# Block 0 ahead of the routers' tables, vectors loaded during layer 0's pages, and first pages of layer 1 cut into pieces inside the fused pass

## The chip, the cores and the metric

One core of a Trainium2 chip runs the whole program. The metric is the device time of one execution in microseconds, without a profile; the median of several runs is given. A profile of one further execution shows where the time goes.

## The reference

Two layers, each of a graph step and a mixture of experts, on 128 graphs of 64 nodes with 256 features (8192 tokens), all in float32:

```python
# layer 0: graph step, then a "lattice" mixture with the best 6 of 64 experts
x = x + gnn0(layernorm(x), adj)       # agg = eps*h + adj@h;  W1 -> rmsnorm -> silu -> W2 (256 -> 1024 -> 256)
x = x + ffn0(layernorm(x))            # sum over 6 experts of score * (h @ lattice[e]), out_w, layernorm
# layer 1: graph step, then a mixture with the best 2 of 8 experts
x = x + gnn1(layernorm(x), adj)       # layer_norm, adj@h@W_rel + h@W_root, relu
x = x + ffn1(layernorm(x))            # relu(h@W1[e]+b1)@W2[e]+b2, weighted with a softmax of the two logits
```

The tokens are routed: only the chosen experts are computed for a token.

## The kernel before

The tokens are worked on in NB = 32 blocks of 256 (two tiles of 128 rows). There are four passes, one after the other, and three seams between them.

1. **Layer 0's graph step** (lines 636 to 870). For each block: load x and its adjacency (`load0`), layer norm (`norm_a`, `norm_s`, `norm_e`, `norm_b`), `aggregate`, four `hidden` parts, `rms`, `scale`, `project`, and then the routing: logits, `choose`, `count`, `place`, and `send`, which scatters the rows of a token to the places of its six experts in a table in DRAM. A `Router` object (r0 for layer 0, r1 for layer 1) keeps small tables for this: its constructor writes them with GpSimd and converts them on VectorE.
2. **Layer 0's pages** (lines 875 to 975). A page is up to 128 rows of one expert. Twelve early pages first, then pairs of pages: `fetch` a page from the table (12 pairs ahead), `flip` (transpose, copy out on ScalarE), `apply` (multiply with the expert's matrix, scale on VectorE, `reply`: scatter the answers to DRAM with an indirect DMA of GpSimd). While the first 64 pairs run, ScalarE's queue also writes filler rows (`fill_end`).
3. **The fused pass** (lines 983 to 1284). For each block: load the six answers per token (`load_y`) and the saved rows (`load3`), sum the answers on TensorE (`mixture`), the output projection, layer norms, layer 1's graph step, and layer 1's routing with `choice`, `count1`, `slots`, `place1` and `send1`. `READY` says for how many first blocks `load_y` need not wait for the last replies; `fold` adds two of the six answers on VectorE in later blocks.
4. **Layer 1's pages** (lines 1287 to 1360). A page is up to 256 rows of one of 8 experts. `fetch1` loads the page, its expert's W1 with b1 (`pw`) and b2; `flip1` transposes; `up` and `down` are the two matrix products; `down` also does the softmax weight and adds the answer to the output with two indirect DMAs that accumulate (`r1.add`). Which expert and which rows a page has is read from a page table that VectorE computes after the last block (`page_table`). The first `FIRST` = 3 pages, numbered -3 to -1, are the first full pages of experts 0 to 2 and need no table. The tiles come from a pool with a fixed number of buffers: four for the page (`px`), three for `pw`, four for b2.

Within a pass, the order on TensorE, VectorE and ScalarE is the program's own: `staggered(n, stages)` takes steps s, and in each step goes through the list of stages, running stage f with lag l for block s - l. So what stands in the list above something else is ahead of it in each engine's order, and an engine takes its instructions strictly in that order. SP's and GpSimd's instructions are placed by the framework's scheduler, which can pull a load forward. SP and ScalarE both issue DMAs; the framework gives these DMAs eight completion semaphores in turn, and a DMA that gets one in use waits until the DMA before it on that semaphore has landed.

The lines that matter:

- Start: the routers are built at lines 616 to 618, ahead of everything of block 0. `load0(0)`, `load0(1)` (lines 659, 660), epsilon, `eye` (epsilon times the identity, line 664), W1 (line 666), b1, and at line 825 a load of ScalarE's function table. After that the `staggered` list with block 0's normalization at lag -1.
- Seam between layer 0's pages and the fused pass: lines 988 to 998 load three weight matrices, Wg and six vectors (ln_g, ln_b, gamma, beta, bg, bias) on ScalarE's queue, and VectorE adds bias to bg. SP loads the answers at line 1010.
- Seam between the fused pass and layer 1's pages: the list ends with `place1` (one `send1`; the other three stand at lag 4), then `page_table`, then the pages with `stages = (-2, fetch1), (0, flip1), (1, down), (0, up)`.

Of the kernel before, what the change touches and what calls it, by code (L numbers as in the profile page):

```python
# [9 lines left out]
F32 = mybir.dt.float32  # L10
# [3 lines left out]
ENG = mybir.EngineType  # L14
# [5 lines left out]
P = 128  # L20
# [509 lines left out]
def two_layer_gnn_moe_kernel(ctx: ExitStack, tc: tile.TileContext, a: dict, out: bass.AP):  # L530
# [16 lines left out]
    READY = 5  # L547
# [92 lines left out]
    with tc.tile_pool(name="c0", bufs=1) as c0, \  # L640
# [10 lines left out]
        r0.begin(counts, work, route)  # L651
# [166 lines left out]
        def load_lattice(b):  # L818
# [6 lines left out]
        nc.scalar.preload_act_table_set("natural_log_exp_and_others")  # L825
# [6 lines left out]
            (-1, norm_a),  # L832
# [3 lines left out]
            (-1, norm_s),  # L836
            (-1, norm_e),
# [6 lines left out]
            (-1, norm_b),  # L844
# [6 lines left out]
            (-1, aggregate),  # L851
# [63 lines left out]
    with tc.tile_pool(name="wx0", bufs=3, reuse_waits="tile") as wx, \  # L915
# [5 lines left out]
        ring = [wx.tile([P, KD, C], F32, name="pxT", bufs=5)]  # L921

# [44 lines left out]
        staggered(mean_pages, stages)  # L967
# [14 lines left out]
    wx = ctx.enter_context(tc.tile_pool(name="wx1", bufs=2, side="right", reuse_waits="tile"))  # L982
    with tc.tile_pool(name="c3", bufs=1, reuse_waits="tile") as c3, \
# [19 lines left out]
        FIRST = 3  # L1003
# [215 lines left out]
        A, H, R, S = chain(output), chain(choice), chain(residual), chain(slots)  # L1219
        staggered(NB, (  # L1220
# [11 lines left out]
            (4, lambda b: send1(b, 1)),  # L1232
# [9 lines left out]
            (1, flip_h),  # L1242
            (2, R),
# [9 lines left out]
            (4, lambda b: send1(b, 2)),  # L1253
# [9 lines left out]
            (4, lambda b: send1(b, 3)),  # L1263
            (1, convolve_a),
            (3, count1),
            (-3, fold),
# [6 lines left out]
            (2, flip3),  # L1273
            (1, convolve_b),
            (2, gate1),
            (0, A),
# [6 lines left out]
        r1.page_table(work.tile([P, 512], F32, name="scratch", bufs=1))  # L1283


    with tc.tile_pool(name="pt4", bufs=2, space=PSUM, reuse_waits="tile") as pt_pool, \
            tc.tile_pool(name="ph4", bufs=4, space=PSUM, reuse_waits="tile") as ph_pool, \
            tc.tile_pool(name="py4", bufs=2, space=PSUM, reuse_waits="tile") as py_pool:
        PG = 2 * P
        pages = {i: dict() for i in range(-FIRST, r1.pages)}  # L1290
        regs = {}

        likely = r1.likely_pages - FIRST

        def load1(i, e):
            Q = pages[i]
            Q["w"] = w = wx.tile([P, F1W], F32, name="pw", bufs=3)
            nc.sync.dma_start(out=w, in_=fw1[ds(e, 1)].rearrange("o p f -> p (o f)"))
            Q["b2"] = b2 = wx.tile([P, D], F32, name="pb2", bufs=4)
            nc.sync.dma_start(out=b2, in_=a["L1_ffn_b2"][ds(e, 1), :].to_broadcast([P, D]))  # L1300

        def fetch1(i):
            Q = pages[i]
            Q["x"] = x = wx.tile([P, 2, W], F32, name="px", bufs=4)
            if i < 0:
                if i == -FIRST:
                    regs["first"] = r1.load_first(0, ENG.SP)
                r1.fetch_first(regs["first"][i + FIRST], x)
                load1(i, i + FIRST)
                return  # L1310
            if i % 4 == 0 or i == likely:
                regs["row"], regs["esp"] = r1.load(0, i, ENG.SP), r1.load(1, i, ENG.SP)
            r1.fetch(i, regs["row"][i % 4], x)
            load1(i, regs["esp"][i % 4])

        def flip1(i):
            Q = pages[i]
            pt = pt_pool.tile([P, KD, PG], F32, name="pt")
            ops.transpose(pt, Q["x"])
            Q["xT"] = xT = wx.tile([P, KD, PG], F32, name="pxT")  # L1320
            nc.scalar.copy(xT, pt)

        def up(i):
            Q = pages[i]
            w = Q["w"]
            Q["hid"] = hid = wx.tile([P, KF, PG], F32, name="phid")
            for c in range(KF):
                ph = ph_pool.tile([P, PG], F32, name="ph")
                for k in range(KD):
                    nc.tensor.matmul(ph, lhsT=w[:, k * F1 + c * P:k * F1 + (c + 1) * P], rhs=Q["xT"][:, k, :],  # L1330
                                     start=(k == 0), stop=(k == KD - 1))
                nc.scalar.activation(hid[:, c, :], ph, AF.Relu, bias=w[:, KD * F1 + c:KD * F1 + c + 1], scale=1.0)  # L1332

        def down(i):
            Q = pages[i]
# [4 lines left out]
            e = regs["e"][i % 4] if i >= 0 else i + FIRST  # L1340

            p = wx.tile([P, 2], F32, name="p")
            nc.scalar.activation(p, Q["x"][:, :, D + 1], AF.Exp)  # L1343
            nc.vector.tensor_scalar(p, p, 1.0, None, op0=ALU.add)  # L1344
            nc.vector.reciprocal(p, p)
            py = py_pool.tile([P, 2, D], F32, name="py")
            y = wx.tile([P, 2, D], F32, name="py_s")
            for t in range(2):
                for c in range(KF):
                    nc.tensor.matmul(py[:, t, :], lhsT=Q["hid"][:, c, ts(t, P)],  # L1350
                                     rhs=fw2[:, ds(e, 1), c, :].rearrange("p o d -> p (o d)"),
                                     start=(c == 0), stop=(c == KF - 1))
            nc.vector.tensor_add(y, py, Q["b2"].unsqueeze(1).to_broadcast([P, 2, D]))  # L1353
            for t in range(2):
                nc.vector.tensor_scalar(y[:, t, :], y[:, t, :], p[:, t:t + 1], None, op0=ALU.mult)
                r1.add(i, Q["x"][:, t, :], y[:, t, :])
# [37 lines left out]
```

## Time and profile before

| | us |
|---|---|
| median of 3 runs without a profile | 2033.03 (2029.64 to 2033.41) |
| the profiled execution, whole | 2284.81 |
| its span, first to last instruction | 2283.0 |
| mean granted clock of TensorE in it | 0.946 |

The four passes in the span, read from the order of time: layer 0's graph step to about 740, layer 0's pages to about 1379, the fused pass to about 1753, layer 1's pages to the end. Busy time in the whole span: PE 87%, PEld 74%, DVE 51%, ACT 44%, POOL 51%.

The profile names the engines PE (TensorE's matmuls), PEld (its weight loads), DVE (VectorE), ACT (ScalarE), POOL (GpSimd), SP (SyncE). A `q` behind a name is the engine's queue that issues DMAs. A line of the view of time gives start and duration in us, the engine, the source line, the instruction, `out<-in` by the program's names without buffer numbers, how many were merged, and in brackets how long the engine was idle before and what released it. In a view of waits the three numbers are total us, count and the longest.

Two rows of the page that the steps below use:

```profile
L386 POOL DMA_INDIRECT out_x<-py_s,px x138 | 215.5, 1561 | 296.4 <-DMA out_x<-py_s,px 235.5
L1330 PE MATMUL ph<-pxT,pw 128*128 128x256 f32 x1104 | 251.3, 381 | 0.7 <-issue 0.7
```

The first is the scatter-add of layer 1's answers: 138 of them (two for each of 69 pages), 1561 ns each, with POOL idle for 296.4 us before them, most of it until an earlier one had landed. The second is `up`: 16 records a page.

### The profile page before, as it was taken

The numbers are of one execution on the slowest core, as the hardware profiler recorded it, in microseconds if no ns is written. First come the engines' busy times: TensorE is split into PE (matmuls) and PEld (weight loads), VectorE is DVE, ScalarE is ACT, GpSimd is POOL, SyncE is SP. The second block draws the span as 40 slices with busy tenths as digits, with TensorE's granted clock in tenths as the row PEclk, the third lists the DMA queues.
The fourth block names the chain that finished last, engine by engine and source line by source line (L and its number), as shares of the span: only waits on it lengthen the run. The fifth ranks groups of instructions, "written<-read, shape, count | busy, mean of one in ns | idle before, by whom it ended". The sixth has DMA issues, their size and how long they took to land. (4 is left out here: it accounts for less than half of the span.)

```text
span 2283.0 us, 36780 instructions
## 1 busy us (share of the span) xinstructions
PE 1975.4 (87%) x10324; PEld 1692.3 (74%) x10324; DVE 1162.4 (51%) x4165; ACT 1007.1 (44%) x2033; POOL 1171.0 (51%) x1134
## 2 busy tenths in 40 slices
PE   7988888888874677888788787999998999999996
PEld 6867777777763566667667666878886888888885
DVE  5868878777876222222222223878996222222221
ACT  5867677676761112121111112666665333333332
POOL 0445566556556666666666662334545344444443
PEclk9999999999996898999989888999998999999998
DMA  4323444444345787755555527999872766766674
GB/s 111 98 100 126 143 144 139 140 140 134 111 159 188 220 246 208 224 176 173 175 172 174 155 73 275 313 305 311 303 227 96 176 168 158 167 163 162 159 163 98
DMA packets 282558, 397.88 MB, mean 174 GB/s; under 512 B 56024, under 2 KB 236392, under 8 KB 282352
## 3 DMA queue, kind: packets, MB, share of 16 engines
q1 hardware_dynamic: 202880, 246.61, 37.0%
q0 software_dynamic: 64416, 136.14, 19.9%
q10 hardware_dynamic: 15056, 12.69, 1.7%
q8 instruction: 92, 1.51, 0.3%
q14 instruction: 114, 0.93, 0.1%
HBM read 222.84 MB, written 176.64 MB: 175 GB/s over the span
## 5 line engine op out<-in xcount | busy, mean ns | idle before, releaser
L369 POOL DMA_INDIRECT r0x<-xs,r0row x384 | 396.9, 1034 | 343.2 <-DVE xs L328 132.8
L954 PE MATMUL py<-lat,pxT 128*128 x1616 | 426.9, 411 | 110.7 <-ACT pxT L941 68.9
L376 POOL DMA_INDIRECT r0y<-px x404 | 391.8, 970 | 227.6 <-DVE px L958 118.9
L954 PEld LDWEIGHTS py<-lat,pxT 128*128 128x128 f32 x1616 | 317.7, 207 | 165.3 <-ACT pxT L941 77.7
L958 DVE TENSOR_SCALAR px<-py,px 128x256 f32<-128x256 f32 x404 | 170.9, 478 | 446.9 <-remote 154.3
L386 POOL DMA_INDIRECT out_x<-py_s,px x138 | 215.5, 1561 | 296.4 <-DMA out_x<-py_s,px 235.5
L941 ACT COPY pxT<-pt 128x512 f32<-128x512 f32 x202 | 113.9, 588 | 515.1 <-remote 214.3
L1332 ACT ACTIVATE phid<-ph,pw 128x256 f32<-128x256 f32 x276 | 130.6, 473 | 323.3 <-issue 186.2
L1330 PE MATMUL ph<-pxT,pw 128*128 128x256 f32 x1104 | 251.3, 381 | 0.7 <-issue 0.7
L1350 PE MATMUL py<-fw,phid 128*128 (+1 forms) x1104 | 249.9, 379 | 0.0
L753 PE MATMUL ps<-lat 128*128 128x256 f32 x1024 | 245.5, 390 | 0.0
L720 PE MATMUL ph<-lat 128*128 128x256 f32 x1024 | 237.5, 390 | 5.1 <-DVE lat L742 2.8
L1330 PEld LDWEIGHTS ph<-pxT,pw 128*128 128x128 f32 x1104 | 210.9, 191 | 30.0 <-issue 1.1
L720 PEld LDWEIGHTS ph<-lat 128*128 128x128 f32 x1024 | 196.9, 195 | 35.7 <-issue 7.0
L1350 PEld LDWEIGHTS py<-fw,phid 128*128 128x128 f32 x1104 | 204.4, 190 | 25.2 <-issue 0.3
L753 PEld LDWEIGHTS ps<-lat 128*128 128x128 f32 x1024 | 198.5, 196 | 26.8
L369 POOL DMA_INDIRECT r1x<-xs,r1row x128 | 137.7, 1076 | 106.5 <-ACT hn L1105 49.8
L939 PE MATMUL pt<-ident,px 128*128 128x128 f32 x808 | 130.7, 283 | 15.7 <-DMA px<-r0x 10.4
L939 PEld LDWEIGHTS pt<-ident,px 128*128 128x128 f32 x808 | 106.6, 148 | 41.3 <-issue 18.5
L723 ACT ACTIVATE lat<-ph,c_L_gnn_b 128x256 f32<-128x256 f32 x256 | 101.2, 471 | 58.5 <-PE ph L720 39.7
L1353 DVE TENSOR_TENSOR py_s<-py,pb 128x512 f32<-128x512 f32 x69 | 47.7, 691 | 155.3 <-PE py L1350 155.3
L1344 DVE TENSOR_SCALAR p<-p 128x2 f32<-128x2 f32 x69 | 11.7, 170 | 224.6 <-ACT p L1343 224.6
(307 smaller groups left out, 2927.2 us busy)
## 6 DMA issues: line engine op xcount, KB each, us to landing
px<-r0x SPq DMA_DIRECT2D x404, 129.0 KB
y<-r0y SPq DMA_DIRECT2D x64, 768.0 KB
pw<-in_L_ffn_W1b SPq DMA_DIRECT2D x69, 514.0 KB
px<-r1x SPq DMA_DIRECT2D x69, 258.0 KB
x<-x SPq DMA_DIRECT2D x64, 256.0 KB
pb<-in_L_ffn_b SPq DMA_DIRECT2D x69, 128.0 KB
r0x<-r0filler ACTq DMA_DIRECT2D x64, 129.0 KB
lat<-in_x SPq DMA_DIRECT2D x32, 256.0 KB
```

The lines of the kernel that those rows point to most:

```text
L369: i = self.nc.gpsimd.indirect_dma_start(out=self.table[:, :], out_offset=bass.IndirectOffsetOnAxis(ap=row[:, t, k:k + 1], axis=0), in_=xs[ ...
L376: d = self.nc.gpsimd.indirect_dma_start(out=self.answer[:, :], out_offset=bass.IndirectOffsetOnAxis(ap=x[:, self.D:self.D + 1].bitcast(I32 ...
L386: i, d = f"{self.name}add{i}", self.nc.gpsimd.indirect_dma_start(out=self.total[:, :], out_offset=bass.IndirectOffsetOnAxis(ap=x[:, self.D ...
L720: nc.tensor.matmul(ph[:, c, :], lhsT=w1[:, k, ts(2 * j + c, P)], rhs=B["aggT"][:, k, :], start=(k == 0), stop=(k == KD - 1))
L753: nc.tensor.matmul(B["po"][:, t, :], lhsT=B["hT"][:, c, ts(t, P)], rhs=w2[:, c, :], start=False, stop=(t == T - 1 and c == KH - 1))
L939: nc.tensor.transpose(pt[:, k, ts(q, P)], Q["px"][:, q, ts(k, P)], ident)
L941: nc.scalar.copy(xT[:, :, :n * P], pt[:, :, :n * P])
L954: nc.tensor.matmul(py[:, q, :], lhsT=xT[:, k, ts(q, P)], rhs=lat[:, ds(regs["e"][(2 * j + q) % 4], 1), k, :].rearrange("p o d -> p (o d)") ...
L958: nc.vector.tensor_scalar(px[:, q, :D], py[:, q, :], px[:, q, D + 1:D + 2], None, op0=ALU.mult)
L1330: nc.tensor.matmul(ph, lhsT=w[:, k * F1 + c * P:k * F1 + (c + 1) * P], rhs=Q["xT"][:, k, :], start=(k == 0), stop=(k == KD - 1))
L1332: nc.scalar.activation(hid[:, c, :], ph, AF.Relu, bias=w[:, KD * F1 + c:KD * F1 + c + 1], scale=1.0)
L1350: nc.tensor.matmul(py[:, t, :], lhsT=Q["hid"][:, c, ts(t, P)], rhs=fw2[:, ds(e, 1), c, :].rearrange("p o d -> p (o d)"), start=(c == 0), s ...
```

## The change

It does four things, in three places.

1. The routers are built after block 0's normalization and aggregation instead of before. Block 0's stages are called once by hand, and the list skips them for block 0 (`rest`). ScalarE's function table is loaded before W1's load is issued, and block 1's loads stand after W1 and b1.
2. The six vectors go into tables of r0 that are no longer needed once layer 0's page table exists, and are loaded during pairs 8 to 13 of layer 0's pages on ScalarE's queue; bias is added at pair 18. `READY` becomes 6, and the condition of `fold` is adapted so that it holds for the same blocks.
3. `FIRST` becomes 4. The functions of a page move ahead of the fused pass and are split: `up` can do a part of its four chunks, `down` one of its two tiles, and `share` and `answer` hold what `down` did on ScalarE, VectorE and GpSimd. Page -4 and the flip and up of page -3 stand in the list of the fused pass at fixed steps, with PSUM tiles borrowed from that pass (`places_of`). After the pass come the page table and then the rest of pages -4 and -3 and the up of page -2.
4. In the last two blocks `place1` sends all four rows of the block at once.

```diff
-    READY = 5
+    READY = 6
...
-    r0 = Router(tc, const, small, dram, N, D, E0, K0, T, P, 14 * P, 4, "r0", 3)
-    W = r0.W
-    r1 = Router(tc, const, small, dram, N, D, E1, 2, T, 2 * P, N, 4, "r1", 1, total=out, like=r0)
-
+    W = D + 2
...
         load0(0)
-        load0(1)
         epsilon = c0.tile([P, 1], F32, name="epsilon")
         nc.scalar.dma_start(out=epsilon, in_=rows_of(a["L0_gnn_epsilon"]))
         eye = c0.tile([P, P], F32, name="eye")
-        nc.vector.tensor_scalar(eye, ident, epsilon, None, op0=ALU.mult)
+        nc.scalar.preload_act_table_set("natural_log_exp_and_others")
...
         b1 = load_columns(c0, "L0_gnn_b1")
+        load0(1)
...
-        nc.scalar.preload_act_table_set("natural_log_exp_and_others")
+        norm_a(0)
+        norm_s(0)
+        nc.vector.tensor_scalar(eye, ident, epsilon, None, op0=ALU.mult)
+        norm_e(0)
+        norm_b(0)
+        aggregate(0)
+        rest = lambda f: lambda b: f(b) if b else None
+
+        r0 = Router(tc, const, small, dram, N, D, E0, K0, T, P, 14 * P, 4, "r0", 3)
+        r1 = Router(tc, const, small, dram, N, D, E1, 2, T, 2 * P, N, 4, "r1", 1, total=out, like=r0)
+        assert W == r0.W
+        r0.begin(counts, work, route)
...
+        over = dict(ln_g=r0.map.rearrange("p j e -> p (j e)")[:, :D], ln_b=r0.nth.rearrange("p j e -> p (j e)")[:, :D],
+                    gamma=r0.end[:, :KD], beta=r0.delta[:, :KD], bg=r0.alloc[:, :E1], gbias=r0.none[:, :E1])
+
+        def load_vectors(j):
+
+            if 8 <= j < 14:
+                name, v = (("ln_g", "L0_ffn_ln_g"), ("ln_b", "L0_ffn_ln_b"), ("gamma", "L1_gnn_ln_gamma"),
+                           ("beta", "L1_gnn_ln_beta"), ("bg", "L1_ffn_bg"), ("gbias", "L1_ffn_bias"))[j - 8]
+                with nc.allow_non_contiguous_dma(reason="small vector"):
+                    nc.scalar.dma_start(out=over[name], in_=a[v].rearrange("(c p) -> p c", p=P) if j in (10, 11)
+                                        else rows_of(a[v]))
+            if j == 18:
+                nc.vector.tensor_add(over["bg"], over["bg"], over["gbias"])
...
-        staggered(mean_pages, stages)
+        staggered(mean_pages, (*stages, (0, load_vectors)))
...
+    FIRST = 4
...
+    def up(i, lo=0, hi=KF):
...
+    def down(i, e, tiles=(0, 1)):
...
+    def share(i):
+
+        Q = pages[i]
+        Q["p"] = p = wx.tile([P, 2], F32, name="p")
+        nc.scalar.activation(p, Q["x"][:, :, D + 1], AF.Exp)
+        nc.vector.tensor_scalar(p, p, 1.0, None, op0=ALU.add)
+        nc.vector.reciprocal(p, p)
+
+    def answer(i):
+        Q = pages[i]
+        y, p = wx.tile([P, 2, D], F32, name="py_s"), Q["p"]
+        nc.vector.tensor_add(y, Q["py"], Q["b2"].unsqueeze(1).to_broadcast([P, 2, D]))
+        for t in range(2):
+            nc.vector.tensor_scalar(y[:, t, :], y[:, t, :], p[:, t:t + 1], None, op0=ALU.mult)
+            r1.add(i, Q["x"][:, t, :], y[:, t, :])
...
-        ln_g = load_rows(c3, "L0_ffn_ln_g")
-        ln_b = load_rows(c3, "L0_ffn_ln_b")
-        gamma = load_columns(c3, "L1_gnn_ln_gamma")
-        beta = load_columns(c3, "L1_gnn_ln_beta")
+        ln_g, ln_b, gamma, beta, bg = (over[x] for x in ("ln_g", "ln_b", "gamma", "beta", "bg"))
...
-        bg = load_rows(c3, "L1_ffn_bg")
-        gbias = load_rows(c3, "L1_ffn_bias")
-        nc.vector.tensor_add(bg, bg, gbias)
...
-            if b > READY + 2:
+            if b > READY + 1:
...
         def place1(b):
-            send1(b, 0)
+            for i in range(4 if b >= NB - 2 else 1):
+                send1(b, i)
...
+        def ahead(*work):
+
+            def do(b):
+                for n, f in work:
+                    if n == b - NB:
+                        f()
+            return do
...
             (1, flip_h),
+            (4, ahead((-4, lambda: up(-4, 0, 2)))),
             (2, R),
...
             (3, count1),
+            (4, ahead((-3, lambda: down(-4, 0, (0,))), (-2, lambda: up(-3)))),
...
             (2, flip3),
+            (4, ahead((-5, lambda: flip1(-4)), (-3, lambda: flip1(-3)))),
             (1, convolve_b),
             (2, gate1),
+            (4, ahead((-8, lambda: fetch1(-4)), (-7, lambda: fetch1(-3)), (-6, lambda: fetch1(-2)),
+                      (-4, lambda: up(-4, 2)), (-3, lambda: down(-4, 0, (1,))))),
...
         r1.page_table(work.tile([P, 512], F32, name="scratch", bufs=1))
+        share(-4)
+        answer(-4)
+        flip1(-2)
+        down(-3, 1)
+        up(-2)
+        share(-3)
+        answer(-3)
...
-        stages = (-2, fetch1), (0, flip1), (1, down), (0, up)
-        staggered(likely, stages, -FIRST)
+        stages = (-2, fetch), (0, then(flip1)), (1, finish), (0, then(up))
+        staggered(likely, stages, -2)
```

In the pages' loop `finish` does what `down` did (`share`, `down`, `answer`, and for pages 0 to 7 the filler), and `then` and `fetch` skip what pages -4 to -2 have already had.

More of the change, by code (lines that the diff above doesn't have):

```diff
@@ L650, in two_layer_gnn_moe_kernel @@
         blocks = [dict() for _ in range(NB)]
-        r0.begin(counts, work, route)
         def load0(b):
@@ L831, in two_layer_gnn_moe_kernel @@
             (-2, lambda b: load0(b) if b > 1 else None),
-            (-1, norm_a),
+            (-1, rest(norm_a)),
             (0, lambda b: hidden(b, 0)),
@@ L835, in two_layer_gnn_moe_kernel @@
             (2, residual_s),
-            (-1, norm_s),
-            (-1, norm_e),
+            (-1, rest(norm_s)),
+            (-1, rest(norm_e)),
             (4, lambda b: send(b, 3)),
@@ L843, in two_layer_gnn_moe_kernel @@
             (2, residual_b),
-            (-1, norm_b),
+            (-1, rest(norm_b)),
             (4, lambda b: send(b, 4)),
@@ L850, in two_layer_gnn_moe_kernel @@
             (0, square_sum),
-            (-1, aggregate),
+            (-1, rest(aggregate)),
             (-1, load_late),
@@ L982, in two_layer_gnn_moe_kernel, with load1 @@
     wx = ctx.enter_context(tc.tile_pool(name="wx1", bufs=2, side="right", reuse_waits="tile"))
+    PG = 2 * P
+    FIRST = 4
+    pages = {i: dict() for i in range(-FIRST, r1.pages)}
+    regs = {}
+    likely = r1.likely_pages - FIRST
+    def load1(i, e):
+        Q = pages[i]
+        Q["w"] = w = wx.tile([P, F1W], F32, name="pw", bufs=3)
+        nc.sync.dma_start(out=w, in_=fw1[ds(e, 1)].rearrange("o p f -> p (o f)"))
+        Q["b2"] = b2 = wx.tile([P, D], F32, name="pb2", bufs=4)
+        nc.sync.dma_start(out=b2, in_=a["L1_ffn_b2"][ds(e, 1), :].to_broadcast([P, D]))
@@ new lines, in fetch1 @@
+    def fetch1(i):
+        Q = pages[i]
+        Q["x"] = x = wx.tile([P, 2, W], F32, name="px", bufs=4)
+        if i < 0:
+            if i == -FIRST:
+                regs["first"] = r1.load_first(0, ENG.SP)
+            r1.fetch_first(regs["first"][i + FIRST], x)
+            load1(i, i + FIRST)
+            return
+        if i % 4 == 0 or i == likely:
+            regs["row"], regs["esp"] = r1.load(0, i, ENG.SP), r1.load(1, i, ENG.SP)
+        r1.fetch(i, regs["row"][i % 4], x)
+        load1(i, regs["esp"][i % 4])
@@ new lines, in flip1 @@
+    def flip1(i):
+        Q = pages[i]
+        pt = Q["pt"](0)
+        ops.transpose(pt, Q["x"])
+        Q["xT"] = xT = wx.tile([P, KD, PG], F32, name="pxT")
+        nc.scalar.copy(xT, pt)
+    def up(i, lo=0, hi=KF):
+        Q = pages[i]
+        w = Q["w"]
+        if lo == 0:
+            Q["hid"] = wx.tile([P, KF, PG], F32, name="phid")
+        hid = Q["hid"]
+        for c in range(lo, hi):
+            ph = Q["ph"](c)
+            for k in range(KD):
+                nc.tensor.matmul(ph, lhsT=w[:, k * F1 + c * P:k * F1 + (c + 1) * P], rhs=Q["xT"][:, k, :],
+                                 start=(k == 0), stop=(k == KD - 1))
+            nc.scalar.activation(hid[:, c, :], ph, AF.Relu, bias=w[:, KD * F1 + c:KD * F1 + c + 1], scale=1.0)
@@ new lines, in down @@
+    def down(i, e, tiles=(0, 1)):
+        Q = pages[i]
+        if 0 in tiles:
+            Q["py"] = Q["py"](0)
+        py = Q["py"]
+        for t in tiles:
+            for c in range(KF):
+                nc.tensor.matmul(py[:, t, :], lhsT=Q["hid"][:, c, ts(t, P)],
+                                 rhs=fw2[:, ds(e, 1), c, :].rearrange("p o d -> p (o d)"),
+                                 start=(c == 0), stop=(c == KF - 1))
+    def share(i):
+        Q = pages[i]
+        Q["p"] = p = wx.tile([P, 2], F32, name="p")
+        nc.scalar.activation(p, Q["x"][:, :, D + 1], AF.Exp)
+        nc.vector.tensor_scalar(p, p, 1.0, None, op0=ALU.add)
+        nc.vector.reciprocal(p, p)
@@ L983, in two_layer_gnn_moe_kernel @@
+    def answer(i):
+        Q = pages[i]
+        y, p = wx.tile([P, 2, D], F32, name="py_s"), Q["p"]
[3 more added lines that the diff above has]
+            r1.add(i, Q["x"][:, t, :], y[:, t, :])
     with tc.tile_pool(name="c3", bufs=1, reuse_waits="tile") as c3, \
@@ L1002, in two_layer_gnn_moe_kernel @@
         pg = pmix.tile([P, T, E1], F32, name="pg")
-        FIRST = 3
         r1.begin(counts, work, pmix.tile([P, 2, T, E1], F32, name="pos"))
@@ L1219, in two_layer_gnn_moe_kernel, with places_of, half @@
         A, H, R, S = chain(output), chain(choice), chain(residual), chain(slots)
+        def places_of(i):
+            def half(c):
+                if c % 2 == 0:
+                    pages[i]["two"] = (po_pool.tile([P, T, D], F32, name="po") if c % 4 == 2 else
+                                       psum.tile([P, KD, C], F32, name="ps"))
+                return pages[i]["two"][:, c % 2, :]
+            pages[i].update(pt=lambda c: psum.tile([P, KD, C], F32, name="ps"), ph=half,
+                            py=lambda c: po_pool.tile([P, T, D], F32, name=("pz", "pc")[i % 2]))
+        def ahead(*work):
[4 more added lines that the diff above has]
+            return do
+        for i in (-4, -3, -2):
+            places_of(i)
         staggered(NB, (
@@ L1231, in two_layer_gnn_moe_kernel @@
             (0, A),
-            (4, lambda b: send1(b, 1)),
+            (4, lambda b: send1(b, 1) if b < NB - 2 else None),
             (0, A),
@@ L1252, in two_layer_gnn_moe_kernel @@
             (0, A),
-            (4, lambda b: send1(b, 2)),
+            (4, lambda b: send1(b, 2) if b < NB - 2 else None),
             (3, H),
@@ L1262, in two_layer_gnn_moe_kernel @@
             (0, A),
-            (4, lambda b: send1(b, 3)),
+            (4, lambda b: send1(b, 3) if b < NB - 2 else None),
             (1, convolve_a),
             (3, count1),
+            (4, ahead((-3, lambda: down(-4, 0, (0,))), (-2, lambda: up(-3)))),
             (-3, fold),
@@ L1288, in two_layer_gnn_moe_kernel, with places_in, finish @@
             tc.tile_pool(name="py4", bufs=2, space=PSUM, reuse_waits="tile") as py_pool:
[L1289 to L1335, printed above, removed]
+        def places_in(i):
+            pages[i].update(pt=lambda c: pt_pool.tile([P, KD, PG], F32, name="pt"),
+                            ph=lambda c: ph_pool.tile([P, PG], F32, name="ph"),
+                            py=lambda c: py_pool.tile([P, 2, D], F32, name="py"))
+        def finish(i):
             if 0 <= i < E1:
@@ L1339, in down, with then, fetch @@
                 regs["e"] = r1.load(1, i, ENG.PE)
[L1340 to L1356, printed above, removed]
-        stages = (-2, fetch1), (0, flip1), (1, down), (0, up)
-        staggered(likely, stages, -FIRST)
+            share(i)
+            down(i, regs["e"][i % 4] if i >= 0 else i + FIRST)
+            answer(i)
+        def then(f):
+            return lambda i: f(i) if i > -2 else None
+        def fetch(i):
+            places_in(i)
+            if i > -2:
+                fetch1(i)
+        stages = (-2, fetch), (0, then(flip1)), (1, finish), (0, then(up))
+        staggered(likely, stages, -2)
         with tc.If(r1.needed(likely)):
```

## Prediction

> **What bounds the kernel now.** I read the page first (span, chain, PE row), then busy time by stretches, then the order of time around the three seams that the edits touch, then the queue's own waits.
>
> The start, in order of time (start, duration, engine, line, instruction, idle before and its releaser):
>
> ```profile
> 5.53 1.28 ACT L825 ACT_TABLE_LOAD   x1 [5.53 <-DMA lat<-in_x]
> 7.77 0.42 DVE L45 BATCH_NORM_STATS2 bn_st<-lat 128x6 f32<-128x256 f32 x1
> 10.06 2.07 PE L710 MATMUL ps<-at,lat 128*128 128x128 f32 x8 [10.06 <-DVE lat L702]
> 12.81 9.48 PE L720 MATMUL ph<-lat 128*128 128x256 f32 x32 [0.68 <-ACT lat L713]
> ```
>
> x of block 0 had landed before 5.53 (ACT's queue was released by it at 5.12), yet its statistics begin at 7.77: VectorE worked on the routers' tables until then.
>
> The seam into the fused pass, as waits of SP's queue from 1370 to 1420 (who, for whom: us, times, longest), and then stretches (PE, PEld, DVE, ACT, POOL busy; PE clock, DMA share, GB/s):
>
> ```profile
> SPq L1010 <- DMA r_L_ffn_ln_g<-in_L_ffn_ln_g: 7.8, 1, 7.8
> SPq L1010 <- DMA r_L_ffn_bias<-in_L_ffn_bias: 2.5, 1, 2.5
> ...
> 1380.00:1383.80 3.80, 0.00 (x0) 0.02 (x1) 0.00 (x0) 0.00 (x0) 2.89 (x4) 0.50 0.93 304
> 1383.80:1387.60 3.80, 2.80 (x13) 2.41 (x13) 0.00 (x0) 0.00 (x0) 1.39 (x2) 0.50 0.92 283
> 1387.60:1394.60 7.00, 2.82 (x12) 2.43 (x13) 0.00 (x0) 0.58 (x1) 0.61 (x3) 0.50 0.88 258
> 1394.60:1400.00 5.40, 5.27 (x24) 4.88 (x25) 0.33 (x3) 0.00 (x0) 0.00 (x0) 0.51 0.94 363
> ```
>
> The loads of block 1's answers (L1010) don't read ln_g, but in the built program they reuse its completion semaphore, so SP stands 7.8 us for it; meanwhile the DMA moves 258 to 304 GB/s, not the 363 to 401 that follow.
>
> The seam into layer 1's pages, and those pages: stretches, then SP's waits from 1755 on, then SP and POOL in order of time.
>
> ```profile
> 1735.00:1744.70 9.70, 8.55 (x43) 6.67 (x44) 4.24 (x27) 4.94 (x10) 4.38 (x7) 0.82 0.24 83
> 1744.70:1753.00 8.30, 3.48 (x20) 2.74 (x20) 4.71 (x38) 2.40 (x4) 5.88 (x6) 0.70 0.32 111
> 1753.00:1760.50 7.50, 6.83 (x28) 5.48 (x28) 5.04 (x33) 2.00 (x4) 5.64 (x6) 0.65 0.32 109
> ```
>
> ```profile
> SPq L515 <- DMA out_x<-py_s,px: 348.6, 81, 6.6
> ```
>
> ```profile
> 1764.46 0.39 SPq L515 DMA_DIRECT2D px<-r1x  x1
> ...
> 1837.53 0.38 SPq L515 DMA_DIRECT2D px<-r1x  x1
> ```
>
> ```profile
> 1765.88 1.62 POOL L386 DMA_INDIRECT out_x<-py_s,px  x1 [5.21 <-DVE py_s L1355]
> ...
> 1797.01 1.55 POOL L386 DMA_INDIRECT out_x<-py_s,px  x1 [5.16 <-DMA out_x<-py_s,px]
> ```
>
> TensorE is idle half of 1744.7 to 1753 and slowed to 0.65 to 0.82. From 1754.85 it is never idle (245.00 of 245 us): 69 pages at 7.347 us. But there is a second, nearly equal clock: each page's two scatter-adds (L386) wait for those of the page before to land, and the fetch of page i (L515) waits for the adds of page i-4, whose buffer it takes. I set each fetch against its page's transposes (page 0 at 1774.95, then every 7.347): the lead is 10.5 us for page 0, falls to 3.5 for page 9 (1837.53) while the fillers are written (adds 8.0 to 8.6 us apart), and stays at 3.5 to 5.7 to the end.
>
> **What the Trainium skill says.** "TensorE: Matmul & The Clock Gate", Part 1 (the HAM clock gate): an idle PE falls back to half clock and comes back after about 3.4 us of activity. The trace agrees in kind: 0.65 to 0.70 above, and the first up projection at 1754.85 takes 5.41 us where later ones take 3.45 to 3.62. "DMA: Bandwidth & Descriptors", Anatomy of one DMA: a DMA has about 2 us that don't depend on size, mostly the receipt of the write. Here a fetch issued at 751.80 let PE go at 754.12 (2.3 us), and the last pages' adds release the next ones 3.1 to 3.2 us after their issue ends. "ScalarE: Activation LUTs", What ACT_TABLE_LOAD costs: about 1.28 us; the trace has 1.28.
>
> **The change, part by part**, in the time of the profiled execution (2284.81 us; span 2283.0). That is 12% above the median of 2033.03 without a profile. The extra must lie mostly where the trace shows PE idle for several us with no releaser (before 1372); layer 1's pages have no such gaps. I take the savings at the seams over unchanged.
>
> *Start.* Block 0's statistics, identity, normalization and aggregation go ahead of the 13 table operations on VectorE, and W1's issue goes behind an ACT table load. Statistics can begin at about 4.6 (landed between 3 and 5.12). From statistics to first matmul took 10.06 - 7.77 = 2.3; identity (0.28, formerly ahead) nearly fits beside ScalarE's rstd: first matmul at 7.0. From there to the hidden layer 12.81 - 10.06 = 2.75: 9.8, against 12.81, gain 3.0. W1 landed by 8.03 (SP's gate load waits for it); 1.28 later is 9.3, just hidden; if it comes at 10.9 the gain is 1.9, and with x at 4.0 it is 3.6. The tables (4.2 us of VectorE) now run from 7.7 to 12, beside matmuls; the next block's normalization waits for its adjacency until 15.24 anyway. SP's and ACT's order is otherwise the same.
>
> *Vectors.* Six small loads and one wait leave the seam at 1379. Block 1's loads go out at about 1380.8 instead of 1387.78, up to 7.0 earlier; what then limits is bandwidth. From 1380 to 1394.6 the DMA moved 3.8 x 0.304 + 3.8 x 0.283 + 7.0 x 0.258 = 4.04 MB; at 380 GB/s, between the 363 and 401 of the next stretches, that takes 10.6 us: gain 4.0. Bounds: 1 (the engines were already 0.88 to 0.93 busy) and 7. The bias wait (VectorE at 1398.12) goes too, but PE's first output projection comes only at 1399.92, behind block 1's answers. In the pages of layer 0 the loads cost ScalarE's queue six issues of about 0.45 beside 0.58 us copies, with ACT busy 17 to 19%: nothing, if their waits don't hold a copy. READY 5 to 6 lets block 5's load off the last replies; these had landed by 1391.57, that load left at 1408.18: nothing. FOLD's condition is the same blocks as before.
>
> *Pieces.* Page -4 whole and the up half of page -3 go into the last steps of the fused pass. All pages stay 69. PE's order gets, before the last count: a flip (0.6), half an up (1.73), half an up (1.73), half a down (1.73), a flip (0.6), half a down (1.73), 8.1 in all. Beside idle time: the second half-up (PE idle until 1747.47) and about 1.1 of the first, most of the last half-down, one flip. On the path: flip 0.6, 0.6 of the first half, half a down 1.7, 0.4 of the last, and ScalarE's two relus (0.47 each) ahead of block 31's deviation, which then starts at about 1747.4 instead of 1745.82: 1.3 more. That is 4.6, less what a warmer PE gives back (pz 3.01 for 1.89, gate 1.88 for 1.06, together 1.9): the page table ends d = 2.8 late, bounds 0 and 8. Then PE would be a page (7.35) ahead. But pages -4 to -1 now hold all four page buffers, so page 0 is fetched only after the adds of page -4, which come after the page table on VectorE: adds at 1765.88 + d, second issue ends 3.5 later, lands 3.1 after that, fetch 3: 1775.5 + d, with no lead where before it was 10.5. While fillers are written the adds come 8.4 apart, and PE must follow: about 1 us a page for four pages. Page 8 starts at 1775.5 + 8 x 7.347 + 4 + d = 1838.3 + d, against 1833.7. Gain 7.35 - 4.6 - d = 2.8 - d = 0. By the chain of adds alone: 69 in both, the first d later, four instead of three of them before the fillers slow it, about 1.6 saved: d - 1.6 = 1.2 lost. I take 0, bounds +6 and -6. POOL's sends are the same number; the last two blocks' four at once fill gaps of under 1 us.
>
> Sum: 3.0 + 4.0 + 0 = 7.0: 2277.8 profiled, 2033.0 - 7.0 = **2026.0** shown.
>
> **The rivals.** A: the pages gain too, because without the profile the adds land sooner and page 0 isn't late. For it: PE-bound all through the pages. Against: 81 fetches released by adds. Then 5 more: 2021. B: the fused pass's start is bound by the DMA whatever the order; shares of 0.88 to 0.94 speak for it, the lower rate against. The vectors give 1, and d is 2 longer: 2031. C, slower: the chain of adds replaces TensorE as the bound of the pages. Its distance is already 6.7 to 8.6 us, mean 7.34 from page 9 to 65, and the lead that absorbed it is gone. Each 0.2 us longer per page costs 65 x 0.2 = 13: 2039; from 0.17 (11 / 65) it is slower than before by 0.2%. Against: the same bytes move. D, the vector loads hold ScalarE: the fillers on that queue held a copy for 13.8 us in four waits, 3.4 each; six such would be 20, so 2046; it decides from four of six. With 64 fillers and four waits this is rare.
>
> **How the numbers follow.** Forecast 0.48, A 0.20, B 0.17, C 0.12, D 0.03. What can be told from no change is 0.2%, 4.1 us. Forecast (2021 to 2030): faster 0.44, same 0.04. A: faster. B: faster 0.05, same 0.10, slower 0.02. C: same 0.02, slower 0.10. D: slower. Together faster 0.69, same 0.16, slower 0.15. The range goes down to 2015 (A with the upper bounds of start and vectors) and up to 2034, which leaves out most of C and D.
>
> **What would show it.** Start: first hidden matmul at 9 to 10.9. Vectors: the loads of the answers wait for no vector; PE's first output projection 3 to 5 us nearer to the end of layer 0's pages. Pieces: page table 0 to 8 us later after the pass's last step; page 0's fetch behind adds with a lead of about 3; short PE idle in pages 0 to 8. I am wrong if PE is never idle there (A), if adds stand over 7.5 apart after page 9 (C), or if ScalarE's copies wait for a vector load (D).

## The result, and the profile after

The changed kernel takes 2026.45 us (median of 12 runs, 2019.32 to 2032.17), the kernel before on the same chip 2034.30 us (12 runs): a ratio of 0.9964, 95% interval 0.9951 to 0.9977, so 7.3 us faster (4.7 to 10.0). The forecast was 7.0. The sum is right, but by luck: below it turns out that two of its three terms are wrong, and that their errors cancel.

In the profile of before and in all runs from e5 on, every kernel takes about 12% longer, with and without the profiler (the kernel before 2279.66 and 2284.26 us), nearly all of it ahead of the fused pass (layer 0's pages end at 1372 to 1389 us in these spans and at 1124 to 1127 in the others) and for a reason that no run shows, so each run is compared with the kernel before that was measured beside it.

The start of the changed kernel, in order of time (columns as before):

```profile
1.21 1.28 ACT L659 ACT_TABLE_LOAD   x1 [1.21 <-PEq L1459]
1.24 0.41 ACTq L661 DMA_DIRECT2D lat<-in_L_gnn_W  x1
1.31 1.37 SPq L610 DMA_DIRECT2D at<-in_adjT  x2
5.19 0.43 DVE L45 BATCH_NORM_STATS2 bn_st<-lat 128x6 f32<-128x256 f32 x1 [5.19 <-DMA lat<-in_x]
8.64 0.43 DVE L688 TENSOR_TENSOR at<-at,eye 128x256 f32<-128x256 f32 x1 [2.09 <-DMA at<-in_adjT]
9.44 2.08 PE L706 MATMUL ps<-at,lat 128*128 128x128 f32 x8 [9.44 <-DVE lat L698]
12.19 9.86 PE L716 MATMUL ph<-lat 128*128 128x256 f32 x32 [0.68 <-ACT lat L709]
```

Statistics now begin when x lands, 2.6 us sooner. But VectorE then stands 2.09 us for the adjacency, which lands only at 8.6. In before, the same addition had come later and waited for nothing:

```profile
8.85 0.41 DVE L692 TENSOR_TENSOR at<-at,eye 128x256 f32<-128x256 f32 x1
```

The first hidden matmul comes at 12.19 instead of 12.81. W1's load, a megabyte, is issued at 1.24, 0.03 us into the table load that stands ahead of it in the program: the table load hardly delays that issue (it left at 1.21 in before).

The seam into the fused pass: SP's waits from 1120 to 1165 (who, for whom: us, times, longest).

```profile
SPq L1107 <- DMA m_L_ffn_out_wT<-in_L_ffn_out_wT: 5.4, 1, 5.4
...
SPq L1099 <- DMA m_L_gnn_W_rel<-in_L_gnn_W_rel: 4.0, 1, 4.0
...
SPq L1099 <- DMA m_L_gnn_W_root<-in_L_gnn_W_root: 1.7, 1, 1.7
```

No vector is in the list any more. The weight matrices have taken the vectors' place, since by the releasers the answers' loads now share their semaphores, but the waits of 7.8 and 2.5 us became waits of 4.0 and 1.7 (the 5.4 holds a later load). From the first issue of answers to TensorE's first output projection it is 15.75 us (1128.37 to 1144.12), where it was 20.87 (1379.16 to 1400.03).

The seam into layer 1's pages: stretches (columns as before), then the fetch of page 0, the first page that needs the page table, and its flip.

```profile
1494.00:1501.00 7.00, 4.37 (x26) 3.22 (x26) 3.81 (x25) 3.11 (x6) 2.16 (x3) 1.00 0.36 115
1501.00:1508.00 7.00, 6.39 (x40) 5.16 (x38) 3.26 (x28) 1.49 (x4) 5.48 (x6) 1.00 0.37 133
1508.00:1528.00 20.00, 18.02 (x84) 14.94 (x85) 10.94 (x56) 7.60 (x17) 10.38 (x9) 1.00 0.41 95
1528.00:1560.00 32.00, 32.00 (x160) 28.20 (x159) 7.80 (x22) 11.91 (x27) 12.43 (x8) 1.00 0.77 188
```

```profile
1522.45 0.39 SPq L515 DMA_DIRECT2D px<-r1x  x1
```

```profile
1528.17 0.60 PE L89 MATMUL pt<-ident,px 128*128 128x128 f32 x4
```

TensorE has its full clock in these stretches (0.65 to 0.82 before). From page 0 (1528.17) to its last matmul it is idle for 0.1 us in all. The fetch of page 0 stands 5.7 us ahead of its flip. In the 20 us ahead of page 0 TensorE is idle for 2 us, and for another reason than I had looked for: each second chunk of an up projection waits 0.56 to 1.08 us until a relu has read the first one out of the PSUM tile that both share. One such wait, from the last steps of the fused pass:

```profile
1497.31 1.13 PE L1048 MATMUL po<-pxT,pw 128*128 128x256 f32 x4 [0.57 <-ACT phid L1050]
```

### The profile page after: what moved, and what is told of

Read it like the earlier page. It is cut to its first block, busy times and chain, and to the rows that moved or that the text cites. A ratio compares the mean times of both kernels' runs of the same rounds, so it can differ in the third digit from the quotient of the medians.

```text
span 2030.3 us, 36761 instructions
## 1 busy us (share of the span) xinstructions
PE 1898.1 (93%) x10324; PEld 1648.7 (81%) x10324; DVE 1169.2 (58%) x4165; ACT 1012.5 (50%) x2033; POOL 1169.7 (58%) x1134
## 5 line engine op out<-in xcount | busy, mean ns | idle before, releaser
L974 PE MATMUL py<-lat,pxT 128*128 x1616 | 388.0, 383 | 18.7 <-ACT pxT L961 15.7
L978 DVE TENSOR_SCALAR px<-py,px 128x256 f32<-128x256 f32 x404 | 177.0, 480 | 311.4 <-PE py L974 307.5
L974 PEld LDWEIGHTS py<-lat,pxT 128*128 128x128 f32 x1616 | 292.6, 191 | 59.7 <-ACT pxT L961 21.3
L1050 ACT ACTIVATE phid<-ph,pw 128x256 f32<-128x256 f32 x264 | 125.2, 474 | 311.5 <-issue 167.0
L1059 PE MATMUL py<-fw,phid 128*128 (+1 forms) x1072 | 242.5, 379 | 0.1
L1048 PE MATMUL ph<-pxT,pw 128*128 128x256 f32 x1056 | 238.7, 379 | 0.0
L749 PE MATMUL ps<-lat 128*128 128x256 f32 x1024 | 238.5, 381 | 0.0
L1048 PEld LDWEIGHTS ph<-pxT,pw 128*128 128x128 f32 x1056 | 200.6, 190 | 27.3
L1059 PEld LDWEIGHTS py<-fw,phid 128*128 128x128 f32 x1072 | 198.5, 190 | 24.6 <-ACT phid L1050 0.3
L369 POOL DMA_INDIRECT r1x<-xs,r1row x128 | 136.9, 1070 | 76.0 <-ACT hn L1194 14.4
L959 PEld LDWEIGHTS pt<-ident,px 128*128 128x128 f32 x808 | 100.9, 142 | 40.1 <-issue 10.0
```

Source lines behind the costliest of these rows:

```text
L369: i = self.nc.gpsimd.indirect_dma_start(out=self.table[:, :], out_offset=bass.IndirectOffsetOnAxis(ap=row[:, t, k:k + 1], axis=0), in_=xs[ ...
L749: nc.tensor.matmul(B["po"][:, t, :], lhsT=B["hT"][:, c, ts(t, P)], rhs=w2[:, c, :], start=False, stop=(t == T - 1 and c == KH - 1))
L959: nc.tensor.transpose(pt[:, k, ts(q, P)], Q["px"][:, q, ts(k, P)], ident)
L974: nc.tensor.matmul(py[:, q, :], lhsT=xT[:, k, ts(q, P)], rhs=lat[:, ds(regs["e"][(2 * j + q) % 4], 1), k, :].rearrange("p o d -> p (o d)") ...
L978: nc.vector.tensor_scalar(px[:, q, :D], py[:, q, :], px[:, q, D + 1:D + 2], None, op0=ALU.mult)
```

## The experiments

All times are medians; a ratio, with its 95% interval, is to the kernel before that was measured in the same set of runs. Each part of the change was first put into the kernel before alone.

**e1: the start alone.** 

> The kernel before with the start edit alone (block 0 ahead of the routers, table load before W1's issue, block 1's loads after W1). The prediction's term: 3.0 us faster (1.9 to 3.6), first hidden matmul at 9.8. The theory from the trace of after: the adjacency of block 0 now lands last, because W1's megabyte is still issued before it; the first hidden matmul comes at about 12.2 (12.81 before), and the kernel is 0.2 to 0.6 us faster, which the times can't tell from nothing.

Measured: 2032.84 against 2032.51 us, ratio 1.0002 (0.9988 to 1.0017). First matmul at 9.43, first hidden matmul at 12.18: as in the changed kernel (12.81 and 12.82 in e2, e3 and e4, which lack this edit). The term of 3.0 us isn't there.

**e2: the vectors alone.** 

> The kernel before with the vectors edit alone (six vectors loaded in layer 0's pages, READY 6). The prediction's term: 4.0 us faster (1 to 7). The theory from the trace of after: 5.0 faster, the way from the first issue of answers to PE's first output projection is 15.8 us instead of 20.8. The rival (bandwidth bounds the seam whatever the order): 1 us faster, that way 19.8.

Measured: 2028.76 against 2032.51 us, ratio 0.9979 (0.9969 to 0.9989), or 4.3 us faster (2.2 to 6.3). From the first issue of answers to the first output projection: 15.3 us. Counted from the end of layer 0's pages, the first output projection comes after 16.6 us in e2 and 17.2 in the changed kernel, against 21.8 in e1 and 21.7 in e3, which have the vectors at the seam. Of these 5 us, 3.2 are left (e2 against e1) at block 0's first matmul with W_rel, and 3.7 to 4.2 (against e3 and e1) at the output projections of blocks 4 to 8, which fits the times. What limits is the DMA: its rate behind the end of the pages (columns as in the stretches of before), first e1, then the changed kernel:

```profile
1132.00:1138.00 6.00, 3.01 (x14) 2.40 (x12) 0.00 (x0) 0.58 (x1) 4.57 (x5) 0.74 1.02 311
1138.00:1145.00 7.00, 4.74 (x23) 4.78 (x24) 0.33 (x3) 0.00 (x0) 5.17 (x7) 0.54 0.93 344
```

```profile
1132.00:1138.00 6.00, 3.90 (x21) 3.60 (x22) 0.00 (x0) 0.00 (x0) 4.47 (x6) 0.56 1.03 387
1138.00:1145.00 7.00, 4.28 (x34) 3.71 (x33) 0.00 (x0) 1.25 (x3) 5.48 (x6) 1.00 1.05 385
```

The rival of 1 us falls. READY, which e2 raises too, isn't the cause: with READY at 5 (e1, e3) block 5's loads leave 48 us behind the end of the pages instead of 27, but around them TensorE waits for answers 0.6 us in e1 and not at all in e3.

**e3: the pieces alone.** 

> The kernel before with the pieces edit alone (FIRST = 4, pages cut up, four sends at once in the last two blocks). The prediction's term: 0 (6 faster to 6 slower), with short idle times of TensorE in pages 0 to 8. The theory from the trace of after: about 2 us faster (1.5 to 3), TensorE never idle from page 0 on; the last count 4.5 to 5 us later after the pass's last step, a page of 7.35 us ahead by then, and 1 us given back behind the last matmul. The rival that the chain of scatter-adds becomes the bound: slower, adds over 7.5 us apart after page 9.

Measured: 2029.95 against 2032.51 us, ratio 0.9984 (0.9973 to 0.9995), or 3.3 us faster (1.0 to 5.5). In the 65 pages from page 0 on TensorE waits for a page twice (0.16 and 0.81 us). The last count comes 41.7 us after the last output projection, against 35.8 in before, and 20.7 us pass between the last matmul and the end. The four sends at once are part of this edit and weren't measured apart.

**e4: the same vectors on another queue.**

```diff
-        ln_g = load_rows(c3, "L0_ffn_ln_g")
+        ln_g = load_rows(c3, "L0_ffn_ln_g", nc.gpsimd)
```

(and the other five likewise). 

> The kernel before with one thing changed: the six vectors are still loaded at the seam into the fused pass, but on GpSimd's queue instead of ScalarE's, so their bytes stay and their place in the turn of completion semaphores goes. If the held semaphore was the cost: the answers' loads wait for no vector and the kernel is 3.5 to 5 us faster, nearly as with the vectors edit. If the bytes were the cost (bandwidth bounds the seam): 0 to 1 us. GpSimd issues the six at 1 us each, after its last replies.

Measured: 2053.11 against 2032.51 us, ratio 1.0097 (1.0076 to 1.0119): 20 us slower. In order of time on GpSimd, and then VectorE's longest wait:

```profile
1168.75 0.97 POOL L376 DMA_INDIRECT r0y<-px  x1 [0.30 <-issue]
1172.95 0.59 POOL L568 DMA_DIRECT2D r_L_ffn_ln_g<-in_L_ffn_ln_g  x1 [3.23 <-DMA r0y<-px]
```

```profile
DVE r_L_ffn_bg L998 <- DMA r_L_ffn_bias<-in_L_ffn_bias: 53.7, 1, 53.7
```

GpSimd still had 35 replies to write when TensorE ended layer 0's pages at 1125.14, 1.28 us each. So the vectors went out 48 us late, and the addition of bias to bg, first on VectorE in the fused pass, held everything. The experiment's time is that of its own mistake. One thing can be read from it: with no vector on ScalarE's queue the first output projection stands 16.3 us after the end of the pages, against 21.8 in e1 and 21.7 in e3. It doesn't separate the semaphore from the bytes, because the bytes had left that stretch as well; but these are 0.27 MB, by estimate 0.7 us at the 385 GB/s above.

**e5: W1 really behind the adjacency** (in the changed kernel).

```diff
-        nc.scalar.dma_start(out=w1, in_=a["L0_gnn_W1"].rearrange("(k p) f -> p k f", p=P))
+        nc.sync.dma_start(out=w1, in_=a["L0_gnn_W1"].rearrange("(k p) f -> p k f", p=P))
```

> The changed kernel with W1's load issued by SP behind x and the adjacency of block 0, instead of by ScalarE beside them. If W1's megabyte is what makes the adjacency land at 8.6: the adjacency lands at about 5, VectorE adds the identity at about 6.6, first matmul at 7.3 to 7.7, first hidden matmul at 10.0 to 10.5, and the kernel is about 2 us faster than the changed one[...]. Rival: W1, 1.5 us later, is then the last to land: first hidden matmul at 11 to 12.2, no gain. Second rival: the megabyte doesn't matter and the small rows of the adjacency are slow by themselves: first matmul still at 9.4.

The start of e5, in order of time:

```profile
1.31 1.37 SPq L610 DMA_DIRECT2D at<-in_adjT  x2
2.73 0.60 SPq L661 DMA_DIRECT2D lat<-in_L_gnn_W  x1
...
6.15 0.42 DVE L688 TENSOR_TENSOR at<-at,eye 128x256 f32<-128x256 f32 x1
...
7.06 2.08 PE L706 MATMUL ps<-at,lat 128*128 128x128 f32 x8 [7.06 <-DVE lat L698]
...
10.29 9.62 PE L716 MATMUL ph<-lat 128*128 128x256 f32 x32 [1.15 <-DMA lat<-in_L_gnn_W]
```

The adjacency is issued at the same time as in the changed kernel and lands over 2.4 us sooner: W1's megabyte, issued ahead of it on another queue, was the cause. Whether its earlier issue or its other queue did it, e5 doesn't separate, since it changes both. The first matmul stands at 7.06, where the prediction had put it, and the first hidden one at 10.29, after 1.15 us for W1. At block 1 the aggregation comes at 19.74, against 21.89 in the changed kernel and 22.13 in before; but it comes at 20.83 in e1, with the changed kernel's start, and at 21.73 to 22.80 in e2 to e4, so that single traces place this gain between 1 and 3 us. Ratio 0.9981 (0.9957 to 1.0006), too wide to show 2 us.

**e6 and e7: two waits of the pieces** (each in the changed kernel). e6 gives each chunk its own PSUM tile, e7 moves a piece to the next step:

```diff
-                if c % 2 == 0:
-                    pages[i]["two"] = (po_pool.tile([P, T, D], F32, name="po") if c % 4 == 2 else
-                                       psum.tile([P, KD, C], F32, name="ps"))
-                return pages[i]["two"][:, c % 2, :]
+                return psum.tile([P, KD, C], F32, name="ps")[:, 0, :]
```

```diff
-            (4, ahead((-4, lambda: up(-4, 0, 2)))),
+            (4, ahead((-4, lambda: up(-4, 0, 2)), (-3, lambda: up(-4, 2)))),
...
-                      (-4, lambda: up(-4, 2)), (-3, lambda: down(-4, 0, (1,))))),
+                      (-3, lambda: down(-4, 0, (1,))))),
```

> The changed kernel with a PSUM tile for each chunk of the up projections of pages -4 to -2, instead of one for two chunks. In the changed kernel TensorE stands 0.56 to 1.08 us in each of six pairs for the relu of the first chunk, 3.9 us in all, 3.4 of them on the way to page 0. If this wait comes from the shared tile: the six waits go, TensorE's last flip before page 0 comes 2.5 to 3.5 us nearer to the pass's last step, and the kernel is up to 3 us faster. Rival: the chain of scatter-adds gives it back behind the last matmul: adds then lag more, end within 1 us of the changed kernel.

> The changed kernel with the second half of page -4's up projection moved in the program to the next step, which leaves TensorE's order as it is and puts ScalarE's two relus behind block 31's deviation instead of ahead of it. The prediction priced the relus ahead of the deviation at 1.3 us on the way to the page table. If so: the deviation starts at 1.5 to 2 us earlier after the pass's last step, VectorE doesn't stand 2.5 us for it, the last count is 0.7 to 2 us earlier, and the kernel is as much faster, or unchanged where the relus then hold the normalization that follows.

e6: ratio 1.0001 (0.9979 to 1.0023). The six waits are gone (the pair of chunks shown above is now one group without a wait):

```profile
1737.42 1.97 PE L1048 MATMUL ps<-pxT,pw 128*128 128x256 f32 x8
```

Page -1's flip stands 11.0 us after the last count instead of 14.4: 3.4 us, as worked out. Then TensorE waits for pages, as it does in e8 (TensorE's waits in layer 1's pages, first e6, then e8):

```profile
PE pt L89 <- DMA px<-r1x: 4.3, 4, 2.4
```

```profile
PE pt L89 <- DMA px<-r1x: 7.3, 8, 1.5
```

From page -1's flip to the last matmul it takes 498 us instead of 489. The gain is given back, and more. e7: ratio 0.9982 (0.9959 to 1.0006). From the moved piece to the last count it takes 8.8 us instead of 10.8, so the relus ahead of the deviation had cost 2.0 us, not 1.3. What follows in this trace is disturbed by two stands of ScalarE and VectorE of 5.1 and 3.1 us that no part of the edit explains, so nothing is read from it behind the count.

**e8: W1, own tiles and late relus together.** 

> The changed kernel with the three edits together: W1 behind the adjacency, own PSUM tiles, relus behind the deviation. If the three gains are on one path and the adds don't give them back: 2 + 3 + 1 = about 5 us below the changed kernel, 2021. If the scatter-adds bound the pages: 2 us below, 2024.

Ratio 0.9975 (0.9954 to 0.9997); the last count is 5.2 us nearer to the last output projection than in the changed kernel, page -1's flip another 2.6 nearer to that, and from there to the last matmul it takes 500 us. The leads of the fetches are 2.7 to 3.4 us in pages 0 to 11 (each page's flip less the issue of its fetch). So by the trace the second reading holds: the scatter-adds bound the pages. The times can't tell 2 us from 5.

**e9 and e10: with and without the pieces.** Both have the vectors, and the start as in e5; e10 is e5's kernel. 

> The kernel before with the start edit (W1 behind the adjacency) and the vectors edit, and without the pieces. It stands against the next run, which has the pieces too. If the pieces are worth the 2.4 us by which TensorE's end comes nearer in the traces: 2 to 4 us slower than the next run. If the scatter-adds give that back behind the last matmul (they end 20 us after TensorE with the pieces and 14 to 20 without): equal to the next run within 1 us. Against the kernel before: 2 to 2.5 for the start and 4 for the vectors, 6 to 6.5 us faster.

> The changed kernel with W1 behind the adjacency, once more, beside the run without pieces on the same chip. If start, vectors and pieces add up: 9 us below the kernel before. If the pieces give nothing: 6 to 6.5.

Ratios 0.9971 (0.9950 to 0.9993) and 0.9966 (0.9943 to 0.9990): by the ratios the pieces make 1 us, with an uncertainty of 7. Inconclusive.

**e11 and e12: the page buffers and the adds** (both in e8's kernel).

```diff
-        Q["x"] = x = wx.tile([P, 2, W], F32, name="px", bufs=4)
+        Q["x"] = x = wx.tile([P, 2, W], F32, name="px", bufs=5)
```

```diff
-            r1.add(i, Q["x"][:, t, :], y[:, t, :])
+            if t == 0:
+                r1.add(i, Q["x"][:, t, :], y[:, t, :])
```

> The version with all three edits and five page buffers instead of four. With four, fetches had a lead of 2.7 to 3 us and TensorE stood for pages (5 to 8 us in all). If the page buffers tie TensorE to the scatter-adds (the prediction's step for page 0): no wait for a page is left, leads of 7 us or more, TensorE's end 5 to 8 us nearer to the last count. If the chain of adds is itself as slow as TensorE, the adds then lag more, the end comes 5 to 8 us later behind the last matmul, and the time is that of four buffers; if it has slack, the kernel is 4 to 6 us faster than with four.

> The version with all three edits (four page buffers), and of the two scatter-adds of each page only the one of the first tile: the answers of the second tile of every page of layer 1 aren't added. If the chain of adds is what holds the pages' fetches and the tail: no wait of TensorE for a page, leads over 8 us, the end 10 to 14 us after the last matmul instead of 20, and 8 us or more off the time. If leads and tail stay, something else holds the fetches.

e11: ratio 0.9924 (0.9890 to 0.9957). TensorE waits for no page; from page -1's flip to the last matmul it is 489 us again. But GpSimd's waits in the pages, first e11, then e12:

```profile
POOL out_x L386 <- DMA out_x<-py_s,px: 247.8, 63, 5.7
```

```profile
POOL out_x L386 <- DVE py_s L1076: 314.4, 55, 6.0
...
POOL out_x L386 <- DMA out_x<-py_s,px: 5.1, 1, 5.1
```

In e11 nearly every page's adds wait for those of the page before to land, and the end comes 25.3 us after the last matmul. The last matmul is 11.0 us nearer to the last count than in e8, and the end 4.3 us farther from it. The leads aren't 7 us or more: they begin at 8.2 and have fallen to 2.9 at page 29. In e12, with one add a page, they wait for the answers themselves; leads grow from 2.7 to 12.7 us, the end comes 8.7 us after the last matmul, and the ratio is 0.9842 (0.9808 to 0.9875). TensorE's part is the same in both (500.8 and 500.7 us from the last count to the last matmul). What the second add of each page costs at the end of e11 is therefore 16.6 us of trace.

The whole way behind the last output projection, from the traces (us; the sums are of unrounded values; the two means are over before, e1, e2, e4, e9 and over the changed kernel, e3, e5, e10):

| kernel | to the last count | to the last matmul | to the end | sum |
|---|---|---|---|---|
| before | 35.8 | 510.4 | 19.6 | 565.8 |
| e2 (no pieces) | 35.8 | 511.2 | 17.3 | 564.2 |
| changed | 40.5 | 503.2 | 20.7 | 564.4 |
| e3 (pieces) | 41.7 | 504.6 | 20.7 | 567.0 |
| mean of five without pieces | 36.0 | 510.9 | 16.8 | 563.8 |
| mean of four with pieces | 40.6 | 503.9 | 20.4 | 564.9 |
| e8 | 35.3 | 511.9 | 21.0 | 568.1 |
| e11 (five buffers) | 37.0 | 500.8 | 25.3 | 563.1 |
| e12 (half the adds) | 37.0 | 500.7 | 8.7 | 546.4 |

Whatever TensorE does, the sum stays at 561 to 568 in all the traces until an add is taken out. With the pieces the last matmul comes 2.4 us sooner, and the end 3.6 us later behind it. Between the first and the last page the adds stand 7.35 us apart in the changed kernel ((2016.45 - 1516.51) / 68) and 7.36 in e11 ((2262.19 - 1761.99) / 68), where TensorE waits for nothing and the adds wait for adds. TensorE's page takes 7.347.

## Why the prediction was right, and where it wasn't

**Start: the step "first matmul at 7.0" failed.** It summed the work between statistics and matmul and left out the wait for the adjacency, which had been hidden behind the routers' tables. The term was 3.0; the trace shows 0.6, the times 0 (2.4 us faster to 3.5 slower). It also took W1's issue to move 1.28 us behind the table load; it moved by 0.03 (from 1.21). e5 shows the rest of the step right: with the megabyte behind the adjacency, 7.06 and 10.29 (7.0 and 9.8 forecast).

**Vectors: right.** Forecast 4.0, measured 4.3 (2.2 to 6.3) alone. The observation named, the first output projection 3 to 5 us nearer to the end of the pages, came out at 5 (16.6 for 21.8 and 21.7). The sum's rate of 380 GB/s is the 385 to 387 that the DMA then moved, and the 4 us are what is left at blocks 4 to 8. Rival B falls with e2. One reading didn't carry over: in the profile of before the last replies ended 9 us behind the pages, in e1 to e4 44 to 46 us behind them, so READY did free block 5's load; that it was worth nothing is still what the waits show. Of rival D, a part happened. ScalarE's waits in the changed kernel, 660 to 720 us:

```profile
ACT pxT L961 <- DMA r0none<-in_L_ffn_bias: 3.2, 1, 3.2
ACT pxT L961 <- DMA r0endrow<-in_L_gnn_ln_gamma: 1.8, 1, 1.8
ACT pxT L961 <- DMA r0delta<-in_L_gnn_ln_beta: 1.8, 1, 1.8
```

Three of the six loads held a copy, 6.8 us in all, where the prediction had put the cost at nothing and the turning point at four. TensorE waited 6.2 us for copies there, against 5.4 in e1 and 4.6 in e3, whose copies waited 4.9 and 5.5 us for filler rows instead: about 1 us. In e2 one load held a copy, for 1.6, and in e5 to e12 none to three did.

**Pieces: the sum of 0 stands in the traces, not in the times.** Right: page 0's fetch waits for the adds of page -4. Right too is that a busier TensorE is granted more clock: in the 16 us from 27.5 us behind the last output projection on, 0.84 to 1.00 in the nine traces with pieces, 0.50 to 0.74 in the five without. The page table is d late within the bounds of 0 to 8: it ends 48.4 us behind the last output projection in the changed kernel and 49.6 in e3, against 43.7 to 45.1 in e1, e2 and e4, so d is 3.3 to 5.9 (2.8 forecast; its own 4.6 less 1.9 is 2.7). At page 0 TensorE is a page more and 4.5 us later than before, so 2.8 us ahead. Mis-sized: the relus (2.0 for 1.3, and the two times that the prediction gives for them differ by 1.6). Missing: the shared PSUM tile (3.4 us up to page 0).

Wrong for the changed kernel: that the fetch comes too late. It left at 1522.45, 1.5 us before what the prediction's sum gives (1765.88 + 2.8 + 3.5 + 3.1, set back by 251.3 us between the two traces: 1524.0), page 0 began 1.2 us after the sum's time, and the lead was 5.7 instead of 3. With the waits for the PSUM tile gone (e6) TensorE is there sooner, the lead is 2.7, and it stands for the page: the bound that the step describes is there, and the overlooked waits had kept TensorE away from it. And the fillers didn't stretch the adds: 7.0 to 8.0 us apart in pages 0 to 8. Why not, these runs don't show. (The 2 us that the prediction takes from the skill stand there for DMAs that GpSimd issues, as the adds are; the fetch at 751.80 that it sets beside them is SP's.)

The times of e3 say 3.3 us gained (1.0 to 5.5). The traces say that the way from the last output projection to the end is no shorter with the pieces: 564.9 on average against 563.8 without. That is near the prediction's "by the chain of adds alone, 1.2 lost", but single traces differ by 3 us or more, too much to confirm it. The profiled executions of the changed kernel and of e3 were slower than their medians (2032.17 for 2026.45; 2032.59 for 2029.95), those of e1 and e2 faster (2030.84 for 2032.84; 2026.69 for 2028.76), and with e10 and e9 it is the other way round, so the traces can't overrule the times. Rival A had supposed that adds land sooner without a profile. This would fit, and was not tested. Where in the kernel the 3 us of e3 are gained stays open, and so does the worth of the pieces, between nothing and 5 us.

So the total was met by luck: by the times the start gave about 3 us less than forecast and the pieces 3.3 more (the three parts alone come to 7.2, the whole measured 7.3). Rival A's observation, no idle TensorE in the pages, is what the trace shows, but not its time of 2021. Rival C isn't what happened to this change: the adds of the changed kernel stand 7.35 us apart. But e6, e8 and e12 show its mechanism, just behind the bound that was left.

e11 has the lowest time of the complete versions, 0.9924 of before. That it beats the changed kernel (0.9964) is not shown: the intervals overlap a little and the sets differ.

## What to carry to other kernels

When work that hid a wait is moved away, list every operand of the first instruction behind it and when each lands: here the small adjacency, not the normalization, was last, and a megabyte issued ahead of it on another queue set its landing. When two chains run at nearly the same pace (7.347 and 7.35 us a page), making one of them shorter moves the wait to the end; measure the other by taking half of it out before tuning the first. And a table load that stands ahead of a DMA issue in the program did not hold it back here: to put a load behind another, issue both from one queue, as e5 does.

## What I had not expected of the hardware

- A DMA issue of ScalarE left at 1.24 us (1.21 in before), 0.03 us into a table load of 1.28 us ahead of it in the program.
- Two adjacency loads of 32 KB each, issued from 1.31 to 2.68, landed at 8.6 beside a megabyte issued at 1.24, and by 6.15 with that megabyte issued at 2.73.
- GpSimd wrote replies until 44 to 46 us after TensorE had ended the pages that they belong to, one every 1.28 to 1.31 us (e1 to e4 and the changed kernel). In e4 a DMA put on its queue at that seam left after all of them.
